# A selective-scan stage rebuilt: one scan per channel group over both state halves, one long buffer for inputs and states, products with C in pairs or trimmed

## The chip, the cores and the metric

The kernel runs on one core of one Trainium2 chip. The metric is the device time of one execution in microseconds (us); the number compared is the median over the timed runs of the same program. Five engines matter here and each works through its own queue in order: TensorE (PE in the profile, its weight loads PEld), VectorE (DVE), ScalarE (ACT), GpSimd (POOL) and SyncE (SP), which issues the DMAs.

## The reference, cut to what matters

The network has four layers. The first three (a gated Fourier block with attention, a Fourier mixing block with experts, a Hartley block) are not touched. The change lies in the fourth, which has two Mamba scans. For both, with `d_state = 16`:

```python
xz = x @ in_w.T
xi, z = jnp.split(xz, 2, axis=-1)
xc = silu(causal_conv(xi) + conv_b)
dt, Bm, Cm = jnp.split(xc @ xproj_w.T, ...)
dt = softplus(dt @ dt_w.T + dt_b)
dA = jnp.exp(dt[..., None] * A)
dBx = dt[..., None] * Bm[:, :, None, :] * xc[..., None]
h = dA_t * h + dBx_t                     # step over time
y = jnp.einsum('bds,bs->bd', h, C_t)
y = (y + xc * D) * silu(z)
return y @ out_w.T
```

The spectral scan ("spe") runs over 8 tokens per pixel, the spatial one ("spa") over all pixels of an image, row after row. Both results go through a group norm and a SiLU, are weighted and added to the layer's input.

## The kernel before

**Tiling.** The scans work in *units*. A spectral unit is 64 pixels of 8 tokens, 512 columns; there are 65. A spatial unit is up to `CR * CW` = 7 rows of 69 columns, 483 columns; an image has 19 of them: a first of 451 columns, 17 of 483 and a last of 170, and there are 4 images. A row's last column stands for a run of constant pixels; the state at the end of such a run comes from one small unit of 60 columns ("run") ahead of the images. The 64 x 2 inner channels and 16 states of a unit do not fit 128 partitions, so each unit is worked in 8 *steps* (`ORDER`, the channel groups q). A step has 128 partitions (channels by 8 states) and two state halves, `sg` 0 and 1.

**A step** takes these operations, for both halves:

- `do_exp` (L1484, ACT): dA = exp(dt * A), one instruction per half, into PSUM. Before, dA has four tiles of one PSUM bank (512 columns), two per step, so that steps take turns in two pairs.
- `do_dB` (L1500): dB = dx * B, both halves at once; for five of eight steps (`BY_DVE`) on DVE from PSUM, where PE has put dx (`do_sel`), for three on POOL from SBUF, where a DMA has put it. dB has its own tile for each q (two of them in a tile called `sr`).
- `do_scan` (L1505, DVE): h = dA * h + dB along the columns, one `tensor_tensor_scan` per half. In spatial units after the first of an image the scan starts from the state in the last column of the unit before.
- `do_hc` (L1532, POOL): hc = h * C for both halves. In spectral units the first of each 8 columns is left out (`do_first` does it by another formula).

**Around the steps**, per unit: `do_x` (PE, then on ACT a table load, two SiLUs and a table load back, L1412 to L1414), `do_dt` in nine parts (softplus out of Relu, Abs, Exp, Ln on ACT; its four terms are summed by PE into `v`, and part 7 copies `v` to dt on ACT, L1441), `do_bc` and `do_keep` (B and C by PE, copied by ACT, L1458), `do_sums` (PE adds hc over the states into y), `do_y` (DVE, yz = y * silu(z), L1557), the output projection. After an image, `combine` normalizes and adds in eight pieces, which lie among the next image's first eight units; each puts another two table loads and two SiLUs on ACT (L1765, L1766) and four copies on DVE (L1778).

**Order.** `scans` writes every operation with a due time in steps (`do(when, ...)`), sorts by it, and issues in that order under `manual_schedule`; equal due times keep the order in which they were written down. Each engine then works in that order and waits at semaphores. What follows names the steps of a unit 0 to 7 in the order in which they run. On ACT the block of `do_x` (due 3.1) lies between the exponentials of step 4 and of step 5 in both kernels. `do_sel` has one PSUM bank: step 0 of the next unit's dx is made (due 5.72) after the DVE has used that of step 7, and it lies on PE ahead of the four matmuls of `v` (due 5.95 to 6.7).

**Carry of the run state.** `keep_run` (L1624) copies the run's last state, per q on DVE, into every dB tile's run columns, once; dB's later writes leave these columns out.

Of the kernel before, what the change touches and what calls it, by code (L numbers as in the profile page):

```python
# [9 lines left out]
F32 = mybir.dt.float32  # L10
BF16 = mybir.dt.bfloat16
AF = mybir.ActivationFunctionType
ALU = mybir.AluOpType
# [4 lines left out]
NB, C, N = 4, 64, 128  # L18
# [5 lines left out]
KW = 65  # L24
ZC = 33
RUN = 60
# [7 lines left out]
CPX = 64  # L34
A1_SIZE = 10 * 4 * CPX + 96
# [277 lines left out]
class Net:  # L313
# [944 lines left out]
    def layer3(self, x2s, x2k, y1, ye):  # L1258
        tc, nc = self.tc, self.nc
        self.x2s, self.x2k, self.y1, self.ye = x2s, x2k, y1, ye  # L1260
        with ExitStack() as ctx:
# [8 lines left out]
            self.dA = [self.psum.tile([128, 512], F32, name=f"dA{i}") for i in range(4)]  # L1270
            self.const, self.small = const, pool("st", 2)
            self.hs = [const.tile([128, 2, 512], F32, name=f"h{q}") for q in range(8)]
# [5 lines left out]
            spare = self.held.tile([128, 32, C], F32, name="sr1").rearrange("p (i s a) c -> p i s (a c)", i=2, s=2)  # L1278
            self.dBs = [const.tile([128, 2, 512], F32, name=f"dB{q}") if q > 1 else spare[:, q] for q in range(8)]
# [8 lines left out]
            for u in us:  # L1288
                u["spa"], u["BC"] = u["kind"] != "spe", [None, None]
                u["c"] = self.consts("spa" if u["spa"] else "spe")  # L1290
# [186 lines left out]
    def do_exp(self, u, q, sg):  # L1477
# [3 lines left out]
        if sg == 0:  # L1481
            self.turn = 2 - self.turn
            u["dA", q] = self.dA[self.turn : self.turn + 2]
        self.nc.scalar.activation(t(u["dA", q][sg][:, u["lo"] : u["n"]]), t(u["dt", q]), AF.Exp, scale=a)  # L1484
# [11 lines left out]
    def do_dB(self, u, q, eng):  # L1496
        lo, dx, dB = u["lo"], u.pop(("dx", q)), self.dBs[q]
# [4 lines left out]
    def do_scan(self, u, q, sg):  # L1502
        lo, n, h = u["lo"], u["n"], self.hs[q][:, sg]
        init = h[:, u["before"] - 1 : u["before"]] if u["before"] else 0.0
        self.nc.vector.tensor_tensor_scan(h[:, lo:n], u["dA", q][sg][:, lo:n], self.dBs[q][:, sg, lo:n], init, ALU.mult, ALU.add)  # L1505
# [22 lines left out]
    def do_hc(self, u, q):  # L1528
        at = slice(u["lo"], u["n"])
        hc = self.work.tile([128, 2, 512], F32, name="hc", bufs=6)[:, :, at]  # L1530
        v = self.later(u, "p s (x t) -> p s x t")
        self.nc.gpsimd.tensor_tensor(v(hc), v(self.hs[q][:, :, at]), v(u["BC"][1][:, :, at]), ALU.mult)  # L1532
        u["hc", q] = hc

    def do_sums(self, u, i):
# [12 lines left out]
        v = self.later(u, "p (x t) -> p x t")  # L1548
        part, sg = divmod(i - 1, 2)
        for q in ORDER[4 * part : 4 * part + 4]:  # L1550
            r, h = divmod(q, 2)
            lhsT = self.c3["sum"][:, 32 * h : 32 * h + 32]
            self.mm(v(u["y"][32 * r : 32 * r + 32]), lhsT, v(u["hc", q][:, sg]), False, i == 4)
# [260 lines left out]
```

## Time and profile before

| what | value |
|---|---|
| timed runs | 7332.48, 7332.04, 7322.53 us; median 7332.04 |
| span of the profiled execution | 7327.9 us; no whole time of that one execution is listed, so it is set beside the median: 4.1 us less |
| scans start / spectral units end / last scan | about 3600 / 5260 / 7262 us of the span |
| engines busy over the whole span | PE 90%, DVE 74%, ACT 65%, POOL 49% |
| DVE scans (L1505) | 2272 instructions |
| POOL products with C (L1532) | 1128 instructions, 2453.5 us |
| spacing of spectral units | 25.58 us (64 spacings) |
| spacing of spatial units without `combine` | 25.27 us (44) |
| spacing of spatial units with `combine` | 27.9 us on average (24) |

The spacings are read off the starts of `dtx` (L1447), which POOL makes once per unit. In the profile, times are microseconds; a group's line has the source line, engine, operation, output and inputs with shapes, the count, the busy time and the mean of one in nanoseconds, and then the engine's idle time just before and what ended it. In a timeline the first column is the start, the second the length, and a bracket at the end gives idle time of that engine and its releaser. A DVE, ACT or POOL instruction's length includes a tail that overlaps the next one, so costs are better read as the distance from one start to the next.

### The profile page before, as it was taken

To read this page: it belongs to the slowest core of one execution; us is meant where nothing else is said; L and a number is where in the kernel's file an instruction comes from. 1 tells how busy PE (TensorE), PEld (TensorE's weight loads), DVE (VectorE), ACT (ScalarE), POOL (GpSimd) and SP (SyncE) were. 2 spreads that over 40 slices of the span, in tenths; PEclk is the share of its full clock that TensorE was granted. 3 is DMA by queue.
4 is the path that set the end of the run, shared out by engine and by line. 5 is a ranking of instruction groups with operands and counts; after the bars stand their busy time and mean duration, and the time that the engine had idled before them with its cause. 6 is when DMAs were issued, how large, how long until landed. Compare 5 with 4: busy or idle time off the path is not lost.

```text
span 7327.9 us, 106846 instructions
## 1 busy us (share of the span) xinstructions
PE 6630.8 (90%) x39058; PEld 2869.5 (39%) x39058; DVE 5405.7 (74%) x7737; ACT 4772.8 (65%) x7768; POOL 3608.7 (49%) x1908
## 2 busy tenths in 40 slices
PE   8998999989999899989899999999899888888897
PEld 6335553347434563346422332222322332332333
DVE  3665546564565646653599999999999899899896
ACT  2564635653455536552588888888788787887885
POOL 1000000000000000000399999999999899899896
PEclk9998989989999989987999999999999999999998
DMA  3000010002000010002455555555455465564554
GB/s 90 1 1 1 28 47 1 1 1 74 1 1 1 28 47 1 1 1 103 141 148 148 150 148 148 150 150 145 132 153 145 131 176 142 143 174 137 155 163 119
DMA packets 364112, 647.03 MB, mean 88 GB/s; under 512 B 46785, under 2 KB 219585, under 8 KB 362049
## 3 DMA queue, kind: packets, MB, share of 16 engines
q1 hardware_dynamic: 357680, 609.91, 30.3%
q10 hardware_dynamic: 5904, 30.28, 1.2%
q8 instruction: 308, 5.05, 0.3%
q14 instruction: 220, 1.79, 0.1%
HBM read 517.80 MB, written 122.22 MB: 87 GB/s over the span
## 4 chain that ended last, share of the span: by engine, by line
PE 49%; DVE 18%; issue 9%; POOL 9%; ACT 9%; DMA 4%; SPq 1%; POOLq 0%; DVEq 0%; ACTq 0%
PE ps_sp L331 14%; PE ps_m L331 9%; DVE h L1505 9%; PE ps_s L331 7%; PE ps_o L331 6%; POOL hc L1532 6%; PE ps_pt L331 4%; DVE dB L1500 3%; PE ps_y L331 3%; PE ps_dx L331 3%; DVE big L1059 2%; ACT dA L1484 2%; DMA s_dx<-ddx 2%; DMA big<-in_sr 1%; PE ps_m L809 1%
## 5 line engine op out<-in xcount | busy, mean ns | idle before, releaser
L1532 POOL TENSOR_TENSOR hc<-h,C 128x966 f32<-128x966 f32 (+3 forms) x1128 | 2453.5, 2276 | 119.7 <-DVE h L1505 92.6
L753 DVE TENSOR_REDUCE nmz<-ps_sp 128x1 f32<-128x320 f32 x2048 | 895.4, 485 | 622.7 <-PE ps_sp L331 613.4
L769 ACT ACTIVATE big<-ps_sp 128x512 f32<-128x512 f32 (+1 forms) x1536 | 830.7, 592 | 719.6 <-PE ps_sp L331 718.3
L928 POOL TENSOR_TENSOR aw<-pack_a 128x128 f32<-128x128 f32 x8 | 3.5, 461 | 2193.5 <-PE ps_m L331 2193.5
L1505 DVE TENSOR_TENSOR_SCAN h<-dA,h,dB 128x483 f32<-128x483 f32 (+2 forms) x900 | 1025.2, 1167 | 52.9 <-ACT dA L1484 52.9
L1505 DVE TENSOR_TENSOR_SCAN h<-dA,dB 128x512 f32<-128x512 f32 (+2 forms) x804 | 929.7, 1188 | 4.0 <-ACT dA L1484 4.0
L331 PE MATMUL ps_sp<-uT,kT 32*128 32x512 f32 x3072 | 924.2, 649 | 1.4 <-ACT big L769 0.8
L331 PE MATMUL ps_dx<-dtx,c_sel 128*128 128x483 f32 (+3 forms) x1420 | 752.7, 612 | 189.5 <-DVE dB L1500 188.3
L1484 ACT ACTIVATE dA<-s_dt,c_spa_a 128x483 f32<-128x483 f32 (+3 forms) x1232 | 760.7, 640 | 178.9 <-DVE h L1505 176.8
L331 PE MATMUL ps_sp<-kT,qT 32*128 32x320 f32 x4096 | 817.3, 499 | 3.9 <-ACT qT L734 3.3
L331 PE MATMUL ps_y<-hc,c_sum 128*32 128x483 f32 (+3 forms) x4512 | 683.7, 561 | 62.7 <-POOL hc L1532 58.0
L1484 ACT ACTIVATE dA<-s_dt,c_spe_a 128x448 f32<-128x448 f32 x1040 | 636.0, 632 | 155.2 <-DVE h L1505 154.3
L1500 POOL TENSOR_TENSOR dB<-s_dx,B 128x952 f32<-128x952 f32 (+6 forms) x300 | 672.6, 2244 | 14.6 <-DMA s_dx<-ddx 7.9
L1500 DVE TENSOR_TENSOR dB<-ps_dx,B 128x952 f32<-128x952 f32 (+4 forms) x600 | 646.0, 1079 | 14.5 <-PE ps_dx L331 13.7
L331 PEld LDWEIGHTS ps_dx<-dtx,c_sel 128*128 128x128 f32 x1420 | 225.4, 190 | 663.7 <-DVE dB L1500 225.4
L331 PEld LDWEIGHTS ps_sp<-uT,kT 32*128 32x128 f32 x3072 | 278.8, 185 | 438.0 <-issue 242.7
L331 PE MATMUL ps_o<-big,va 128*32 128x512 f32 (+1 forms) x3072 | 415.1, 612 | 0.0
L331 PE MATMUL ps_s<-pack_a,big 128*64 128x128 f32 (+4 forms) x2832 | 369.1, 306 | 44.8 <-DMA big<-in_x 19.8
L331 PEld LDWEIGHTS ps_sp<-kT,qT 32*128 32x128 f32 x4096 | 358.1, 190 | 57.2 <-issue 36.6
L331 PEld LDWEIGHTS ps_s<-pack_a,big 128*128 128x128 f32 (+2 forms) x2832 | 328.6, 180 | 66.3 <-issue 25.6
L1505 DVE TENSOR_TENSOR_SCAN h<-dA,h,sr 128x483 f32<-128x483 f32 (+2 forms) x300 | 342.6, 1162 | 0.0
L1500 POOL TENSOR_TENSOR sr<-s_dx,B 128x952 f32<-128x952 f32 (+2 forms) x150 | 336.6, 2246 | 0.3
(406 smaller groups left out, 10968.8 us busy)
## 6 DMA issues: line engine op xcount, KB each, us to landing
s_dt<-ddt SPq DMA_DIRECT2D x520, 256.0 KB
s_dt<-ddt SPq DMA_DIRECT2D x544, 241.5 KB
s_dx<-ddx SPq DMA_DIRECT2D x195, 256.0 KB
s_dx<-ddx SPq DMA_DIRECT2D x204, 241.5 KB
ddt<-dt SPq DMA_DIRECT2D x65, 256.0 KB
ddx<-dtx SPq DMA_DIRECT2D x65, 256.0 KB
A<-x2s SPq DMA_DIRECT2D x136, 121.2 KB
ddt<-dt SPq DMA_DIRECT2D x68, 241.5 KB
```

The source lines that it names most:

```text
L331: self.nc.tensor.matmul(out, lhsT, rhs, start=start, stop=stop)
L753: nc.vector.tensor_reduce(self.nmz[n % 2][:, j, at : at + 1], p[:, :KEYS], AX.X, ALU.max, negate=True)
L769: nc.scalar.activation(slot(m, 2 * wu + q)[rows], p[rows], AF.Exp)
L809: nc.tensor.transpose(p[:, 128 * j : 128 * j + 128], o[:, 128 * j : 128 * j + 128], k("ident"))
L928: nc.gpsimd.tensor_tensor(aw[i], k(f"aw{i + 1}"), k("sg"), ALU.mult)
L1059: nc.vector.scalar_tensor_tensor(acc(i), y, gate[:, p : p + 1], acc(i), ALU.mult, ALU.add)
L1484: self.nc.scalar.activation(t(u["dA", q][sg][:, u["lo"] : u["n"]]), t(u["dt", q]), AF.Exp, scale=a)
L1500: eng.tensor_tensor(v(dB[:, :, x:y]), v(d), v(u["BC"][0][:, :, x:y]), ALU.mult)
L1505: self.nc.vector.tensor_tensor_scan(h[:, lo:n], u["dA", q][sg][:, lo:n], self.dBs[q][:, sg, lo:n], init, ALU.mult, ALU.add)
L1532: self.nc.gpsimd.tensor_tensor(v(hc), v(self.hs[q][:, :, at]), v(u["BC"][1][:, :, at]), ALU.mult)
```

## The change

Two PSUM tiles of 1024 columns (two banks each) take the place of the four of 512, and steps alternate between them. One SBUF tile `all` has for each q one row of 1456 columns (`hd`) that holds both dB and the states. In spectral units dB is written to columns 0 to 1023 and one scan over 1024 columns overwrites it with h; the first column of each 8 has dA = 0, so nothing carries over from one half to the other. In spatial units after the first of an image one scan covers both halves with two carry columns: dA there is 0, and the dB buffer begins 483 columns behind the h buffer, so that the last state of the unit before is read as dB of the carry column. The scan then has 968 columns (655 in an image's last unit). The first unit of an image and the run keep two scans. Since states now overwrite dB's run columns of half 0, `keep_run` moves to ACT and restores them twice per spatial unit from `e_run`. Products with C are made on POOL for two steps at once in spectral units (1792 columns, three buffers for pairs in place of six), and in full spatial units without each row's last four columns (910 in place of 966); PE's sums then have 455 columns in place of 483. Due times: exponentials at -1.3 and -1.0 instead of -1.56 and -1.2, scan at 0.3 instead of 0.1 and 0.5.

```diff
-            self.dA = [self.psum.tile([128, 512], F32, name=f"dA{i}") for i in range(4)]
+            self.dA = [self.psum.tile([128, 1024], F32, name=f"dA{i}") for i in range(2)]
...
+            self.all = const.tile([128, 8, HD], F32, name="hd")
+            self.hd = {q: self.all[:, k] for k, q in enumerate(ORDER)}
...
-            self.turn = 2 - self.turn
-            u["dA", q] = self.dA[self.turn : self.turn + 2]
-        self.nc.scalar.activation(t(u["dA", q][sg][:, u["lo"] : u["n"]]), t(u["dt", q]), AF.Exp, scale=a)
+            self.turn = 1 - self.turn
+            u["dA", q] = self.dA[self.turn]
+        at = (TOK + 1) * sg + 1 if u["spa"] else 512 * sg
...
+        self.nc.scalar.activation(t(u["dA", q][:, at + u["lo"] : at + u["n"]]), t(u["dt", q]), AF.Exp, scale=a)
...
-    def do_scan(self, u, q, sg):
-        lo, n, h = u["lo"], u["n"], self.hs[q][:, sg]
-        init = h[:, u["before"] - 1 : u["before"]] if u["before"] else 0.0
-        self.nc.vector.tensor_tensor_scan(h[:, lo:n], u["dA", q][sg][:, lo:n], self.dBs[q][:, sg, lo:n], init, ALU.mult, ALU.add)
+    def do_scan(self, u, q):
+
+        scan = self.nc.vector.tensor_tensor_scan
+        lo, n, hd, dA = u["lo"], u["n"], self.hd[q], u["dA", q]
+        if not u["spa"]:
+            scan(hd[:, :1024], dA, hd[:, :1024], 0.0, ALU.mult, ALU.add)
+            return
+        if u["carried"]:
+            m = TOK + n + 2
+            scan(hd[:, :m], dA[:, :m], hd[:, TOK : TOK + m], 0.0, ALU.mult, ALU.add)
+            return
...
     def do_hc(self, u, q):
...
+        if u["spa"]:
+            at = slice(u["lo"], u["n"])
+            v = self.kept if u["carried"] and u["n"] == CR * CW else lambda t: t
+            mul(v(hc[:, :, at]), v(h[:, :, at]), v(c[:, :, at]))
+            return
+        if k % 2:
+            later = lambda t: t.rearrange("p i (x t) -> p i x t", t=8)[..., 1:]
+            h = later(self.all[:, k - 1 : k + 1, :1024])
...
-    def keep_run(self, u, q):
-        run = self.hs[q][:, :, RUN - 1].unsqueeze(2).to_broadcast([128, 2, CR])
-        self.nc.vector.tensor_copy(self.dBs[q][:, :, CW - 1 : CR * CW : CW], run)
+    def keep_run(self, u, part):
...
+        self.nc.scalar.copy(runs(0), self.e_run[:, at].to_broadcast([128, 4, CR]))
...
+            for part in range(2 if spa else 0):
+                do(4.1 * part + 4.6, self.keep_run, u, part)
...
-            do(-1.56, self.do_exp, u, q, 0)
-            do(-1.2, self.do_exp, u, q, 1)
+            do(-1.3, self.do_exp, u, q, 0)
+            do(-1.0, self.do_exp, u, q, 1)
...
-            do(0.1, self.do_scan, u, q, 0)
-            do(0.5, self.do_scan, u, q, 1)
-            if u["kind"] == "run":
-                do(0.55, self.keep_run, u, q)
-            else:
+            do(0.3, self.do_scan, u, q)
+            if u["kind"] != "run":
                 do(0.77, self.do_hc, u, q)
```

## Prediction

> **What bounds the kernel now.** I first read busy time by stretch, then, inside one unit, the timelines of POOL, DVE, ACT and PE. The stretches, columns PE, PEld, DVE, ACT, POOL busy, clock, DMA share, GB/s:
>
> ```profile
> 4000.00:4600.00 600.00, 548.80 (x2068) 179.65 (x2068) 578.64 (x564) 490.36 (x752) 600.00 (x306) 1.00 0.56 149
> 5450.00:5653.00 203.00, 183.98 (x610) 57.14 (x610) 193.40 (x182) 162.83 (x266) 203.00 (x98) 1.00 0.51 145
> 6300.00:6800.00 500.00, 435.38 (x1579) 155.36 (x1577) 456.32 (x494) 412.25 (x664) 465.54 (x237) 0.96 0.55 154
> ```
>
> In spectral units (first line) and in spatial units without `combine` (second) POOL has no idle time: it sets the 25.58 and 25.27 us per unit. DVE is at 96 and 95%. In the third stretch, where units with `combine` are mixed in, nobody is full, so something waits in a circle. POOL's starts give its prices:
>
> ```profile
> 4442.65 6.57 POOL L1532 TENSOR_TENSOR hc<-h,C 128x896 f32<-128x896 f32 x3
> 4448.94 2.60 POOL L1500 TENSOR_TENSOR sr<-s_dx,B 128x1024 f32<-128x1024 f32 x1
> 4451.27 1.51 POOL L1447 TENSOR_TENSOR dtx<-dt,xc 128x512 f32<-128x512 f32 x1
> ```
>
> Start to start: hc 2.10 us, dB 2.33, dtx 1.23. From 512 to 1024 columns that is 2.15 ns a column and 0.13 us fixed. Now ACT around `do_x`, and DVE beside it:
>
> ```profile
> 4402.55 0.64 ACT L1484 ACTIVATE dA<-s_dt,c_spe_a 128x448 f32<-128x448 f32 x1 [0.48 <-DVE h L1505]
> 4403.20 1.28 ACT L1412 ACT_TABLE_LOAD   x1
> 4404.49 1.20 ACT L1412 ACTIVATE xc<-ps_m,c_spe_cb 128x512 f32<-128x512 f32 x1
> 4405.48 1.16 ACT L1413 ACTIVATE zs<-ps_m 128x512 f32<-128x512 f32 x1
> 4406.65 1.28 ACT L1414 ACT_TABLE_LOAD   x1
> 4407.94 1.19 ACT L1484 ACTIVATE dA<-s_dt,c_spe_a 128x448 f32<-128x448 f32 x2
> ...
> 4412.55 0.62 ACT L1484 ACTIVATE dA<-s_dt,c_spe_a 128x448 f32<-128x448 f32 x1
> ...
> 4418.91 0.59 ACT L1441 COPY dt<-ps_m 128x512 f32<-128x512 f32 x1 [1.31 <-PE ps_m L331]
> ```
>
> ```profile
> 4400.20 2.31 DVE L1505 TENSOR_TENSOR_SCAN h<-dA,dB 128x512 f32<-128x512 f32 x2
> 4402.43 0.67 DVE L1557 TENSOR_TENSOR yz<-ps_y,zs 128x512 f32<-128x512 f32 x1
> 4403.01 1.21 DVE L1505 TENSOR_TENSOR_SCAN h<-dA,dB 128x512 f32<-128x512 f32 x1
> 4404.14 1.20 DVE L1500 TENSOR_TENSOR dB<-ps_dx,B 128x1024 f32<-128x1024 f32 x1
> ...
> 4408.62 1.22 DVE L1505 TENSOR_TENSOR_SCAN h<-dA,dB 128x512 f32<-128x512 f32 x1
> ...
> 4414.39 1.23 DVE L1500 TENSOR_TENSOR sr<-ps_dx,B 128x1024 f32<-128x1024 f32 x1 [1.20 <-PE ps_dx L331]
> ```
>
> Step 2's second scan ends at 4402.51. That frees the bank for step 4's second exponential (4402.55); then come 4.74 us of table loads and SiLUs, then step 5's first exponential, which ends at 4408.58. Step 5's first scan starts at 4408.62, just when DVE is free for it: slack zero. DVE's only idle time is 1.20 us before step 0's dB, behind PE, which waits for POOL. Where the ACT block is longer, with `combine`, the same place already costs time:
>
> ```profile
> 5920.52 1.22 DVE L1505 TENSOR_TENSOR_SCAN h<-dA,h,dB 128x483 f32<-128x483 f32 x1 [1.87 <-ACT dA L1484]
> ```
>
> **The change, part by part.** *Scans.* The scan's length rises from 252 ns (60 columns) to 1204 (512): 2.106 ns a column. Two of 512 are 2.24 us start to start; one of 1024 should be 2.20 (not under 2.16, columns alone; not over 2.24). Two of 483 with a state as start value are also 2.24, one of 968 is 2.08. Saved on DVE: 0.3 us per spectral, 1.3 per spatial unit. 1096 scans go. A scan across two banks is shown nowhere; I bound an extra price by zero and the 0.04 us fixed part.
>
> The Trainium skill (Perfetto Trace Analysis, "Optimizing Scalar/DVE Operations") gives about 125 ns per DVE instruction on PSUM and advises grouping where the engine is saturated; by that figure 1096 scans would be 137 us and the kernel at an estimated 7195. The rows above give 0.04 to 0.16 us each, and the saturated engine is POOL. The same section says that breaking instructions up may finish work sooner where an engine that isn't saturated causes bubbles in others, and that speaks against this change.
>
> *Products.* A pair saves one fixed part, 0.13 us (bounds 0 and 0.25, should 2 x 128 rows of 7 be worse or better): POOL 25.1 per spectral unit. Trimming 56 columns saves 0.12 us eight times: 24.3 per spatial unit. Rows with gaps cost nothing extra in dB (952 columns in rows of 68: 2.19 us).
>
> *Exponentials.* In the changed program step k's first exponential waits for the whole scan of step k-2, since a half is no tile of its own any more; the second also waits for the first to end (0.66 us start to start, as `sp_w` after `sp_u`, in place of 0.57). So after scan 2 ends ACT runs both exponentials of step 4, the block, and both of step 5, and only then scan 5 may start: 0.045 + 0.67 + 0.65 + 4.74 + 0.67 + 0.64 + 0.045 = 7.46 us. DVE's own work between is yz 0.58, scan 3 2.20, dB 1.12, scan 4 2.20, 0.08 of it already run: 6.02. Scan 5 is 1.4 us late, each unit.
>
> *Behind it.* Step 7's dB starts at 7.46 + 2.20 = 9.66. PE's `do_sel` for step 0, behind it, starts at 11.0 (length 1.20 and 0.14 to PE, as the dB at 4404.14 is followed by PE at 4405.48). From `do_sel` to the dt copy PE needs 5.68 (4413.23 to 4418.91), all matmuls back to back:
>
> ```profile
> 4413.23 1.13 PE L331 MATMUL ps_dx<-dtx,c_sel 128*128 128x512 f32 x2
> 4414.29 0.96 PE L331 MATMUL ps_y<-hc,c_sum 128*32 128x448 f32 x8
> 4415.18 1.13 PE L331 MATMUL ps_m<-sp_c,xht 128*128 128x512 f32 x2
> ```
>
> In the new order the dt copy (due 7.0) stands before step 0's second exponential (now also 7.0, written later; before, 6.8). So scan 0 starts at 11.0 + 5.68 + 0.49 + 0.64 + 0.045 = 17.85. From there to the next scan 2's end: three scans, two dB, 8.9. A spectral unit takes 26.8 us instead of 25.58; 64 of them: **+76**.
>
> If dt were not late: scan 6 waits for its second exponential, 4.04 us of ACT behind scan 5's (4409.13 to 4413.17), so 11.50; then five scans, three dB, y0: 14.6; unit 26.1: +34. That is the floor.
>
> *Spatial units without `combine`,* same sum with their rows (exponentials 0.70 apart with the wait, 0.68 to the load, block 3.74): scan 5 at 6.58, `do_sel` at 9.92, dt 5.50 later, scan 0 at 16.80, 8.4 more, unit 25.2 against 25.27; 44 of them: **-3**. Floor without the dt delay, and POOL's own work: 24.3, -43.
>
> *With `combine`:* from scan 1's end two exponentials and a copy, 4.17 of loads and SiLUs, two exponentials, 3.73, two exponentials: scan 5 at 12.5, scan 0 at 22.7, unit 28.4 against 27.9; 24 of them: **+12** (without the dt delay 27.6: -7).
>
> *`keep_run`.* Two small copies on ACT per unit; the nearest row is the 0.18 us ACT instruction on 7 columns, I take 0.2. The first waits for step 3's product and is reached 8.0 us after scan 2; POOL ends that product between 4.7 (straight after scan 3) and 6.8 (behind its own queue), so it waits for nothing. If POOL were later, exponential 6 behind the copy, and with it scan 6, would be late by as much. POOL's dB for the next step 1 waits for the copy, a product lies between. DVE loses its eight copies in the run unit: nothing. SP's queue keeps its DMAs and their order. An image's last unit scans 655 columns (1.42 us) in place of twice 170 (0.54 us each): up to 4 x 8 x 0.4 = 13 us if DVE binds there; 17 us pass in that unit for some 14 of DVE work, so I take 0.
>
> Sum: 76 - 3 + 12 = +85 on the profiled span of 7327.9: 7413; with the 4.1 us by which the median of the runs lies above it, **7417**. POOL has slack then (25.1 of 26.8), so its gains don't show.
>
> **The rivals.**
>
> - *Floor:* PE gets from scan 5 to dt sooner by 0.7 us or more, so that dt is in time. +34 - 43 - 7 = -16: 7316. For: PE no longer waits for a late POOL. Against: the 5.68 us hold no wait, and dx has one bank.
> - *ACT keeps ahead (the other side):* POOL remains the bound and its savings count: 64 x 0.5 + 44 x 0.97 = -75: 7257. It decides if scan 2 to scan 5 on ACT stays within 6.0 us. Against: zero slack at 4408.62 and 1.87 us at 5920.52.
> - *Pairs are slow:* POOL's unit is four pairs and 8.8 us (three dB, dtx, bb 0.60), so it binds again when a pair takes over 4.5 us in place of 2 x 2.10 - 0.13 = 4.07. Each 0.1 us beyond is 4 x 64 x 0.1 = 26 us; at 4.8 us 7417 + 77 = 7494. Against: rows of 7 already run at (2.10 - 0.13) / 896 = 2.2 ns a column.
> - *More waits:* yz follows dB 3 by one scan only, where PE took 2.5 us from dB 3 to the sums (4399.15 to 4401.64), so yz and the next unit's matmuls slip by 0.4 us; hidden in scan 5's wait until it passes that by another 0.3. At 0.5 us in each of 132 units 7417 + 66 = 7483.
>
> **How the numbers follow.** Forecast 0.72 (its own range 7380 to 7455), floor 0.09, ACT ahead 0.05, slow pairs 0.07, more waits 0.07. The range 7340 to 7480 leaves out the next two and the far half of the last two, 0.2 together. The measurement tells about 0.2%, 15 us. The floor lies just past it, so half of it counts as same: faster 0.10, same 0.06, slower 0.84.
>
> **What would show it.** Right: DVE idle before scans by ACT's dA (now none in spectral units) of 1.4 and more per unit, scan 0 released by the exponential behind the dt copy, POOL no longer at 600 of 600, unit spacing 26.8, 25.2, 28.4; scan 2.20 and 2.08, pair 4.07, trimmed product 2.08 us. Wrong: a spectral spacing under 25.6, or POOL still full.

## The result and the profile after

The changed kernel takes 7570.34 us (median; 7564.79 to 7575.03) against 7332.26 for the kernel before in the runs beside it: 1.0327 times as long, 95% interval 1.0313 to 1.0342. The forecast was 7417, its range ended at 7480: the direction was right, the size was not. The profiled execution has a span of 7562.9 us, 235.0 more than before's.

The same three stretches as before, columns PE, PEld, DVE, ACT, POOL busy, granted clock, DMA share, GB/s:

```profile
4000.00:4600.00 600.00, 514.11 (x1936) 171.52 (x1934) 538.07 (x349) 460.15 (x703) 550.28 (x198) 0.97 0.51 139
5450.00:5653.00 203.00, 170.57 (x576) 55.42 (x574) 178.09 (x113) 158.55 (x268) 189.88 (x93) 0.95 0.49 138
6300.00:6800.00 500.00, 408.47 (x1494) 148.37 (x1486) 419.58 (x337) 397.93 (x664) 424.30 (x224) 0.94 0.52 144
```

POOL is no longer full (550 of 600 instead of 600) and DVE fell from 96 to 90% in spectral units: every engine now waits for another. The clock column (the share of full speed that TensorE was granted) fell too, from 1.00 to 0.97 and 0.95 in the first two rows. The prediction printed that column and drew nothing from it.

Where the waits lie, from the list of costly groups (behind the bar: busy us, mean ns, then the engine's idle time just before and what ended it):

```profile
L1564 POOL TENSOR_TENSOR hc<-hd,C 128x910 f32<-128x910 f32 (+3 forms) x868 | 2316.0, 2677 | 362.3 <-DVE hd L1529 147.5
L1529 DVE TENSOR_TENSOR_SCAN hd<-dA,hd 128x968 f32<-128x968 f32 (+1 forms) x576 | 1226.3, 2131 | 188.7 <-ACT dA L1490 185.9
L333 PE MATMUL ps_dx<-dtx,c_sel 128*128 128x483 f32 (+3 forms) x1420 | 796.1, 644 | 589.9 <-DVE hd L1518 589.5
L1525 DVE TENSOR_TENSOR_SCAN hd<-dA,hd 128x1024 f32<-128x1024 f32 x520 | 1185.2, 2283 | 109.7 <-ACT dA L1490 100.5
```

DVE's scans wait 286 us for ACT, as forecast. PE waits 589.5 us for DVE's dB at `do_sel`, three times the 188.3 us of before.

**One unit.** ACT, DVE and PE in the unit that the prediction worked through and at the start of the next (a timeline: start, length, and in brackets the idle time and its releaser):

```profile
4405.12 1.31 ACT L1490 ACTIVATE dA<-s_dt,c_spe_a 128x448 f32<-128x448 f32 x2 [1.24 <-DVE hd L1525]
4406.44 1.28 ACT L1415 ACT_TABLE_LOAD   x1
...
4411.20 1.31 ACT L1490 ACTIVATE dA<-s_dt,c_spe_a 128x448 f32<-128x448 f32 x2
...
4421.68 0.58 ACT L1444 COPY dt<-ps_m 128x512 f32<-128x512 f32 x1 [2.09 <-PE ps_m L333]
...
4430.03 0.58 ACT L1461 COPY C<-ps_m 128x512 f32<-128x512 f32 x1 [3.18 <-PE ps_m L333]
...
4435.70 1.19 ACT L1415 ACTIVATE xc<-ps_m,c_spe_cb 128x512 f32<-128x512 f32 x1 [0.96 <-PE ps_m L333]
```

```profile
4402.80 2.28 DVE L1525 TENSOR_TENSOR_SCAN hd<-dA,hd 128x1024 f32<-128x1024 f32 x1
...
4412.54 2.29 DVE L1525 TENSOR_TENSOR_SCAN hd<-dA,hd 128x1024 f32<-128x1024 f32 x1 [0.83 <-ACT dA L1490]
...
4416.63 2.29 DVE L1525 TENSOR_TENSOR_SCAN hd<-dA,hd 128x1024 f32<-128x1024 f32 x1 [0.69 <-ACT dA L1490]
...
4422.84 2.29 DVE L1525 TENSOR_TENSOR_SCAN hd<-dA,hd 128x1024 f32<-128x1024 f32 x1 [0.43 <-ACT dA L1490]
...
4429.56 2.28 DVE L1525 TENSOR_TENSOR_SCAN hd<-dA,hd 128x1024 f32<-128x1024 f32 x1
4433.84 0.69 DVE L1605 TENSOR_TENSOR yz<-ps_y,zs 128x512 f32<-128x512 f32 x1 [2.00 <-PE ps_y L333]
...
4440.51 2.29 DVE L1525 TENSOR_TENSOR_SCAN hd<-dA,hd 128x1024 f32<-128x1024 f32 x1 [0.47 <-ACT dA L1490]
```

Scan 2 (4402.80) ends at 4405.08. Step 4's exponentials start 0.04 later, the block and step 5's exponentials follow, and scan 5 starts at 4412.54, 7.46 us behind scan 2: the forecast's 7.46. Scan 6 waits for its exponential (4.09 behind scan 5; 4.04 forecast). Scan 0 starts at 4422.84, released by the exponential behind the dt copy, 10.30 behind scan 5 (10.39 forecast). The chain is there, link by link.

What the chain did not hold is on PE, where this unit passes into the next:

```profile
4416.00 1.12 PE L333 MATMUL ps_dx<-dtx,c_sel 128*128 128x512 f32 x2 [0.52 <-DVE hd L1518]
...
4422.34 1.88 PE L333 MATMUL ps_m<-xc,c_spe_bc 128*128 128x512 f32 x4
4426.30 2.08 PE L333 MATMUL ps_dx<-dtx,c_sel 128*128 128x512 f32 x2 [2.08 <-DVE hd L1518]
4428.17 2.63 PE L333 MATMUL ps_m<-xc,c_spe_bc 128*128 128x512 f32 x4
```

The same dx matmul takes 1.12 us elsewhere, the same B and C matmul 1.88. Three stretches around it (columns as above):

```profile
4415.94:4426.20 10.26, 8.22 (x24) 3.03 (x24) 9.14 (x8) 7.45 (x14) 9.15 (x4) 1.00 0.45 134
4426.20:4429.60 3.40, 3.30 (x4) 1.51 (x5) 3.40 (x4) 0.64 (x1) 3.40 (x3) 0.51 0.87 189
4429.60:4436.40 6.80, 6.80 (x35) 1.89 (x33) 4.80 (x4) 5.36 (x8) 6.80 (x3) 1.00 0.69 192
```

After PE had waited 2.08 us for DVE's dB, its clock was half for 3.4 us (a drop, in what follows). What stands behind on PE comes late: C's copies (ACT idle 3.18 us; 1.52 one unit earlier), the x matmuls (xc idle 0.96; none earlier), the sums (yz idle 2.00; 0.43 earlier). So in this next unit scan 5 (4440.51) comes 8.67 us behind the end of scan 2 (4431.84), not 7.46.

The 57 steady spectral units of this trace, from one scan 2's end to the next, are of three kinds. In 28 no drop meets the chain: 26.7 to 26.8 us, as forecast. In 24 a drop follows the wait for step 2's dB: yz waits 2.0 to 2.1 us for PE, xc 0.96 to 1.13, scan 5 comes 8.7 to 8.8 us behind scan 2, and the unit takes 27.9 to 28.0. In 5 the drop falls on the dx matmul behind z: scan 0 comes 11.4 us behind scan 5 instead of 10.30, and the unit takes 27.7. Plain spatial spacings are of two kinds: 9 of 38 at 25.1 to 25.2, as forecast, and 29 at 26.7 to 26.9. Between 3600 and 5260 us the time at half clock is 106 us in the changed kernel and 14 before; from 5260 to 7300 it is 259 and 167; from 3600 to the end of the last scan, 410 and 161.

**Where the 235 us lie,** from the spacings of `dtx` (here 61 steady spectral spacings, 38 between units without and 21 between units with `combine`):

| | before, us | after, us | sum, us |
|---|---|---|---|
| spectral units | 25.58 | 27.33 | +107, and +6 in the first three |
| spatial without `combine` | 25.28 | 26.40 | +43 |
| spatial with `combine` | 27.91 | 29.61 | +36 |
| images' ends, run, first units (18) | | | +38 |
| ahead of the first and behind the last | | | +6 |

The spectral spacings of `dtx` are not even: most alternate between 26.1 to 26.4 and 28.3 to 28.6 us, and two of them make 54.6 us, which is sixteen times 3.413 us.

### The profile page after: what moved, and what is told of

The parts are those of the page before. It is cut to its first block, busy times and chain, and to the rows that moved or that the text cites. A ratio compares the mean times of both kernels' runs of the same rounds, so it can differ in the third digit from the quotient of the medians.

```text
span 7562.9 us, 105294 instructions
## 1 busy us (share of the span) xinstructions
PE 6622.1 (88%) x39058; PEld 2887.9 (38%) x39058; DVE 5344.1 (71%) x6633; ACT 4813.2 (64%) x7926; POOL 3524.4 (47%) x1648
## 4 chain that ended last, share of the span: by engine, by line
PE 56%; DVE 19%; ACT 11%; issue 7%; POOL 4%; DMA 3%; SPq 0%; DVEq 0%; POOLq 0%; ACTq 0%
PE ps_sp L333 13%; PE ps_m L333 12%; PE ps_s L333 7%; PE ps_o L333 6%; PE ps_dx L333 6%; DVE hd L1518 5%; DVE hd L1525 5%; PE ps_pt L333 4%; PE ps_y L333 4%; ACT dA L1490 3%; DVE hd L1529 3%; POOL hc L1564 2%; DMA big<-in_sr 2%; DVE big L1061 2%; ACT L1417 1%
## 5 line engine op out<-in xcount | busy, mean ns | idle before, releaser
L1564 POOL TENSOR_TENSOR hc<-hd,C 128x910 f32<-128x910 f32 (+3 forms) x868 | 2316.0, 2677 | 362.3 <-DVE hd L1529 147.5
L1529 DVE TENSOR_TENSOR_SCAN hd<-dA,hd 128x968 f32<-128x968 f32 (+1 forms) x576 | 1226.3, 2131 | 188.7 <-ACT dA L1490 185.9
L333 PE MATMUL ps_dx<-dtx,c_sel 128*128 128x483 f32 (+3 forms) x1420 | 796.1, 644 | 589.9 <-DVE hd L1518 589.5
L1525 DVE TENSOR_TENSOR_SCAN hd<-dA,hd 128x1024 f32<-128x1024 f32 x520 | 1185.2, 2283 | 109.7 <-ACT dA L1490 100.5
L1518 POOL TENSOR_TENSOR hd<-s_dx,B 128x1024 f32<-128x1024 f32 (+5 forms) x450 | 956.4, 2126 | 95.1 <-ACT hd L1681 78.5
L1518 DVE TENSOR_TENSOR hd<-ps_dx,B 128x1024 f32<-128x1024 f32 (+5 forms) x750 | 810.9, 1081 | 33.2 <-PE ps_dx L333 31.7
L1490 ACT ACTIVATE dA<-s_dt,c_spa_a 128x483 f32<-128x483 f32 (+3 forms) x1232 | 788.9, 645 | 44.9 <-DVE hd L1529 30.6
L333 PE MATMUL ps_y<-hc,c_sum 128*32 128x455 f32 (+3 forms) x4512 | 548.6, 556 | 3.2 <-POOL hc L1564 3.2
L333 PE MATMUL ps_s<-pack_a,big 128*64 128x128 f32 (+4 forms) x2832 | 371.6, 307 | 43.7 <-DMA big<-in_x 20.2
L333 PE MATMUL ps_m<-xc,c_spa_bc 128*128 128x483 f32 (+3 forms) x616 | 313.1, 631 | 0.0
L1461 ACT COPY C<-ps_m 128x483 f32<-128x483 f32 (+4 forms) x284 | 159.5, 562 | 211.7 <-PE ps_m L333 210.9
```

The costliest lines, as they stand in the source:

```text
L333: self.nc.tensor.matmul(out, lhsT, rhs, start=start, stop=stop)
L1461: self.nc.scalar.copy(u["BC"][k // 2][:, k % 2, u["lo"] : u["n"]], u["bc", k])
L1490: self.nc.scalar.activation(t(u["dA", q][:, at + u["lo"] : at + u["n"]]), t(u["dt", q]), AF.Exp, scale=a)
L1518: eng.tensor_tensor(v(dB[:, :, x:y]), v(d), v(u["BC"][0][:, :, x:y]), ALU.mult)
L1525: scan(hd[:, :1024], dA, hd[:, :1024], 0.0, ALU.mult, ALU.add)
L1529: scan(hd[:, :m], dA[:, :m], hd[:, TOK : TOK + m], 0.0, ALU.mult, ALU.add)
```

## The experiments

**Theory A:** the two-bank dA tile makes a loop over DVE, ACT and PE (26.8 us per spectral unit, 25.2 in plain spatial ones, as forecast), and that loop lets PE idle so long that its clock falls, which adds the rest. **Rivals:** B, PE's order is late whatever its clock is; D, the products' part causes the loss; and, later, that the due times, the long scan, `keep_run` or ACT's order do.

All numbers, with the mean spacings from each profile (spectral / without `combine` / with) and the time at half clock between 3600 and 7300 us (the same window for all, so that it leaves out the last units of the slower kernels):

| kernel | time, us | spacings, us | half clock, us |
|---|---|---|---|
| before | 7332 | 25.58 / 25.28 / 27.91 | 182 |
| after | 7570 | 27.33 / 26.40 / 29.61 | 365 |
| two added matmuls | 7557 | 27.29 / 25.48 / 30.66 | 321 |
| z over 128 rows | 7574 | 27.29 / 26.37 / 29.90 | 352 |
| both | 7492 | 26.68 / 25.37 / 30.20 | 150 |
| dt copy later | 7515 | 27.09 / 25.81 / 28.91 | 333 |
| no table loads (after) | 7567 | 27.30 / 26.35 / 29.92 | 420 |
| products as before | 7592 | 27.31 / 26.52 / 30.08 | 369 |
| before, new due times | 7331 | 25.57 / 25.27 / 27.82 | 195 |
| before, tile and due times | 7496 | 27.32 / 25.35 / 29.52 | 340 |
| before, products | 7281 | 25.21 / 24.53 / 27.92 | 221 |

**1. Keep PE's clock up.** First with two matmuls of zero weights (`FILL` is 2) where PE waits for step 2's dB; `self.open` is the unit whose y PE is summing:

```diff
         self.mm(u["bc", k], u["c"]["bc"][:, 128 * k : 128 * k + 128], u["xc"])
+        if k == 1 and self.open:
+            for _ in range(FILL):
+                self.mm(self.open["y"][0:32], self.zero, self.open["zs"], False, False)
```

> The changed kernel, with two matmuls of zero weights put on PE where it waits for step 2's dB (they add nothing to y). Theory A (the clock): the changed kernel's loop is 26.8 us per spectral unit by its waits, as predicted, and the rest comes from PE running at half clock for 3.41 us whenever it idled for most of the 3.41 us before. Then the time at granted clock 0.5 in 3600 to 5260 us falls from 106 us to under 35, spectral units are 26.8 us each without the alternation of 26.2 and 28.4, plain spatial units come to 25.2, and the whole to 7430 to 7470 us against 7570. Rival B (the order on PE: what stands behind do_sel is late whatever the clock is): spacing and time stay, 7570 within 15.

7557.33 us, ratio 1.0301 to before. Plain spatial units did what A said (29 of the 38 spacings lie at 25.1 to 25.2). Spectral units stayed at 27.3, which B had said, but not for B's reason: the half clock was still there, 133 us of it, and had moved. PE and the clock, in the unit of this kernel:

```profile
4415.52 1.12 PE L334 MATMUL ps_m<-A,c_spe_z 64*128 64x512 f32 x2
4417.92 1.41 PE L334 MATMUL ps_dx<-dtx,c_sel 128*128 128x512 f32 x2 [1.28 <-DVE hd L1522]
4419.27 1.97 PE L334 MATMUL ps_m<-yz,c_spe_ow 128*64 128x512 f32 x2
```

```profile
4415.16:4418.57 3.41, 2.13 (x6) 0.59 (x4) 3.41 (x3) 3.38 (x4) 3.41 (x2) 1.00 0.85 243
4418.57:4421.98 3.41, 3.41 (x5) 0.79 (x4) 2.58 (x2) 2.73 (x4) 3.41 (x2) 0.50 0.03 7
```

In the first of the two stretches PE was busy 2.13 of 3.41 us, and still the clock fell in the next. A third of the stretch was z, a matmul on 64 of 128 rows. Hence the second edit, in which z takes all 128 rows, the added weights zero:

```diff
-        self.mm(v(pz), c["z"][64:128], a2[64:128])
+        self.mm(v(pz), c["z"], a2)
...
+            nc.vector.memset(c3[s + "_z"][0:64], 0.0)
```

> The changed kernel, with the matmul of z over 128 rows in place of 64, the added weights zero; the same columns, so the same time on PE at the same clock. In the run with two added matmuls the half clock moved to the dx matmul behind z, after 3.41-us stretches that were idle for 0.37 only, of which z on 64 of 128 rows filled a third. Theory A2: what sets the clock is work weighed by its share of the 128 rows, with the border near 0.47 of a 3.41-us stretch. Then this alone takes away the drops behind z and leaves those behind the long wait for dB (about 2 us): spectral units stay near 27.3 us and the time within 7540 to 7575. Theory A1 (only idle time counts): no change at all in the number of drops.

7573.85 us: no gain alone, as expected. Drops behind the long wait stay. Both edits together, without the added matmuls in units with `combine`:

> The two matmuls of zero weights in the long wait and z over 128 rows together; the two matmuls are left out where the output of the image before is combined, since there they stood in PE's way (12 of those units took 30 to 33 us in the run with them everywhere, 2 without). Theory A2: time at half clock in spectral units falls from 106 us to under 30, their spacing to 26.1 to 26.8 without alternation (33 to 77 us less), plain spatial units to 25.2 (some 50 less), combine units stay: 7450 to 7495. Theory A1 (only idle time counts): the drops behind z stay as with the two matmuls alone, spectral 27.3, 7520 to 7560. Theory B (order on PE, not its clock): the clock rises and the spacing stays at 27.3 and 26.5, 7570.

7492.20 us, ratio 1.0217 (1.0200 to 1.0234): 78 us back. PE in the same place, and the spectral stretch:

```profile
4421.71 1.02 PE L334 MATMUL ps_m<-xht,c_spe_z 128*128 128x512 f32 x2
4424.21 1.10 PE L334 MATMUL ps_dx<-dtx,c_sel 128*128 128x512 f32 x2 [1.47 <-DVE hd L1523]
4425.23 1.07 PE L334 MATMUL ps_m<-yz,c_spe_ow 128*64 128x512 f32 x2
```

```profile
3600.00:5260.00 1660.00, 1499.19 (x5678) 495.71 (x5679) 1519.90 (x987) 1305.71 (x1987) 1547.30 (x561) 1.00 0.52 141
```

PE idles a little longer behind z (1.47 us), and its matmuls keep full speed: the row count of z decided. Half clock in the spectral part is 7 us instead of 106. The spacing there is 26.68 us and, first units included, the spectral part costs 74 us more than before, where the prediction had 76. On DVE, from scan 2's end to the next, all its steady units take 26.66 to 26.69 us, with scan 5 at 7.46 and scan 0 at 17.76. Plain units have 25.1 in most places, where it had 25.2. So B falls, and so does the view that only idle time counts. The spacings of `dtx` still vary between 26.1 and 27.2 us without any drop; since DVE's units are even, that variation is of POOL's place for `dtx` alone.

**2. The dt copy behind step 0's second exponential.**

```diff
-            do(-1.0, self.do_exp, u, q, 1)
+            do(-1.02, self.do_exp, u, q, 1)
```

> The changed kernel, with one due time altered: the second exponential of a step at -1.02 in place of -1.0, so that on ACT the dt copy comes behind the second exponential of the next unit's step 0. Theory A: the unit has a chain through dt of 26.8 us and one without it of 26.1; scan 0 is then no longer released by an exponential behind dt, and 0.7 us per spectral and 0.9 per spatial unit go (100 us over the 132), less what the clock gives back: 7480 to 7550. Rival C (the dt copy is only late because something else on PE is, and that bounds the unit): the spacing stays at 27.3, time 7570 within 15.

7515.06 us, inside A's range: 55 us for the delay that the prediction had priced at 0.7 to 0.9 us per unit (some 100), with the half clock little changed (333 us in place of 365). In spectral units it gave only 0.24 us, where 0.7 was priced.

**3. The products' part,** alone on the kernel before, and taken out of the changed kernel:

```diff
-        hc = self.work.tile([128, 2, 512], F32, name="hc", bufs=6)[:, :, at]
+        if k % 2 == 0:
+            u["hcs"] = self.work.tile([128, 2, 2, 512], F32, name="hc", bufs=3)
...
+            mul(later(u["hcs"].rearrange("p i s x -> p i (s x)")), h, cc)
```

> The kernel before, with the products' part of the change alone (pairs in spectral units, trimmed in spatial ones; scans, dA and dB as before). Theory A: POOL is the bound of the kernel before, so its savings count: 0.5 us for each of 64 spectral and 0.97 for each of 44 plain spatial units, 75 us, 7257 (7245 to 7285). Rival D: ACT, which had no slack at scan 5 in the trace before, or a pair that comes too late for the sums, takes the gain: 7320 to 7340.

> The changed kernel with products as before the change (each step by itself, 896 and 966 columns). POOL is then at 25.6 of 27.3 us per spectral unit and 25.3 of 26.4 in spatial ones. Theory A: products are hidden in the loop's slack, 7570 within 20. Rival D (the pairs or the trimming are part of the loss): 7500 or less. Rival E (POOL's saving shows already): 7600 or more.

Alone the products make the kernel faster than both: 7280.54 us, ratio 0.9924 (0.9907 to 0.9940), 54 us of A's 75. The stretches of this kernel, columns as above:

```profile
4000.00:4600.00 600.00, 548.98 (x2083) 181.58 (x2082) 587.73 (x572) 499.40 (x762) 596.59 (x214) 1.00 0.56 151
5450.00:5653.00 203.00, 183.81 (x628) 58.75 (x620) 199.70 (x188) 168.62 (x273) 203.00 (x101) 1.00 0.54 149
```

POOL is still all but full and DVE at 98%: where POOL bounds, its savings count, 0.37 and 0.75 us per unit. In the changed kernel they hide: without them it takes 7591.92, 22 us more. That is 2 us beyond the range that A gave, so they show a little. D falls.

**4. ACT's block.** Relu in place of the SiLUs in spectral units takes two table loads out of the block between the exponentials of steps 4 and 5 (and makes the spectral scan another one).

```diff
-        nc.scalar.activation(w(u["xc"]), v(p), AF.Silu, bias=c["cb"])
-        nc.scalar.activation(w(u["zs"]), v(pz), AF.Silu)
-        nc.scalar.preload_act_table_set("natural_log_exp_and_others")
+        F = AF.Silu if first else AF.Relu
+        nc.scalar.activation(w(u["xc"]), v(p), F, bias=c["cb"])
+        nc.scalar.activation(w(u["zs"]), v(pz), F)
```

> The changed kernel, with Relu in place of the two SiLUs of do_x in all spectral units but the first, so that their two table loads go (the spectral scan's output is another one). The block on ACT between the exponentials of steps 4 and 5 shrinks from 4.74 to about 2.2 us. Theory A: scan 5 then waits until 4.9 us behind scan 2, and DVE has 6.0 us of its own work, so ACT no longer holds it; the loop falls to what DVE and POOL need, 25.0 to 25.5 us per spectral unit, PE no longer idles long and keeps its clock: 64 times 1.9 to 2.3 us less, 7425 to 7450. If the two-bank scan were late through something else than this block, the spacing would stay above 26.5 and the time above 7515.

> The same edit on the kernel before, as a control. POOL is full there in spectral units, so without the tables the spacing stays at 25.58 us within 0.1 and the time at 7335 within 12. If ACT was part of the bound before, up to 1 us per unit goes, 7270.

The control stayed (7331.15). The changed kernel stayed too, at 7567.20 with 27.30 us: a clear miss of A. DVE in that kernel:

```profile
4407.44 2.29 DVE L1528 TENSOR_TENSOR_SCAN hd<-dA,hd 128x1024 f32<-128x1024 f32 x1 [1.57 <-ACT dA L1493]
...
4424.18 0.69 DVE L1608 TENSOR_TENSOR yz<-ps_y,zs 128x512 f32<-128x512 f32 x1 [2.12 <-PE ps_y L333]
```

Scan 5 waits no more. In its place scan 6 waits 1.57 us (before the edit 0.69) for an exponential that stands behind softplus on ACT, and yz 2.12 us for PE, which is at half clock for 147 us in the spectral part, 41 more than with the tables. So the block is one link of the loop and not its only price. No run keeps this kernel's clock, but its trace holds units without a drop: 16 of 57 take 26.1 to 26.4 us, the others 27.6 to 27.9. So without drops the block would be worth some 0.6 us (26.7 to 26.1), an estimate from these units; the drops hide it, and A's 25.0 to 25.5 is not reached.

**5. Which part makes the loop.** The tile alone on the kernel before, first with the old due times:

```diff
-            self.dA = [self.psum.tile([128, 512], F32, name=f"dA{i}") for i in range(4)]
+            self.dA = [self.psum.tile([128, 1024], F32, name=f"dA{i}") for i in range(2)]
```

> The kernel before, with only the four one-bank dA tiles made two two-bank tiles (two scans per step, due times and products as before). An exponential then waits for both scans of the step two back. Theory A: step 5's first exponential ends 0.045 + 0.67 + 0.57 + 4.74 + 0.60 = 6.6 us behind scan 2's end, where DVE's own work (yz 0.58, two steps of scans 4.48, dB 1.12) takes 6.2: scan 5 is late by 0.4 to 0.5 us in each spectral unit. POOL, which is full, must take that up, so 25.6 to 26.1 us per unit and 7330 to 7370: the tile alone is not the loss, the whole scan and the late dt copy behind it make the larger part. Rival F (the tile is the loss): 26.5 and more per unit, 7430 and above.

8413.99 us, far from both. This is no measure of the tile: with the old due times the first exponential of step k (-1.56) is written down ahead of the second scan of step k - 2 (-1.5). As the two halves are now one tile, that scan takes the tile to be rewritten and waits for the exponential, and the exponential waits for the first scan. ACT and DVE take turns in each step (one such scan waits 3.27 us for ACT; 33.2 us per spectral unit). With the new due times this goes:

> The kernel before with the changed due times of the exponentials alone (-1.3 and -1.0), four one-bank tiles and two scans per step kept. On ACT the dt copy comes ahead of step 0's second exponential. Theory A: scan 0's second half is then released by that exponential, 16.5 us behind scan 2's end, and 7.9 us of scans and dB follow: 24.4 us, less than POOL's 25.58, so no change: 7332 within 15. Rival J (the due times are the loss): 26.5 us and more per spectral unit, 7400 and above.

> The kernel before with two two-bank tiles and the changed due times, but two scans per step and products as before. Theory A: an exponential waits for both scans of the step two back and the first scan for both exponentials; scan 5 comes 7.3 to 7.5 us behind scan 2's end as in the changed kernel, scan 0 some 17.6 us, and 8.9 us follow: 26.4 to 26.8 us per spectral unit as in the changed kernel, and more where PE's clock drops, 7440 to 7580. Then the tile, not the long scan, is the loss. Rival K (the whole scan is needed for it): 25.6 to 26.0, 7330 to 7370.

The due times alone cost nothing (7330.84, ratio 0.9997, 0.9988 to 1.0007). Tile and due times together, with two scans per step, make 7495.63 us (ratio 1.0220) and the same 27.32 us per spectral unit as the whole change. DVE there shows the same two waits:

```profile
4417.08 1.22 DVE L1505 TENSOR_TENSOR_SCAN h<-dA,dB 128x512 f32<-128x512 f32 x1 [1.27 <-ACT dA L1484]
...
4421.17 1.22 DVE L1505 TENSOR_TENSOR_SCAN h<-dA,dB 128x512 f32<-128x512 f32 x1 [0.62 <-ACT dA L1484]
```

So in spectral units the loss is the tile's: half a step can no longer be freed or released by itself. The rival that the whole scan is needed for it falls. That the mean is 27.32 here and 27.33 in the whole change says little by itself, since ten different kernels of this case share it (see the last section); what counts is that this kernel's units without a drop (27 of 56) take 26.4 to 26.9 us and the others 27.8 to 27.9, much as in the changed kernel. Plain spatial units lose hardly anything by the tile (25.35); their 1.1 us come with the rest of the change, and go again when PE's clock is kept (25.37 in the run with both edits).

**6. Units with `combine` and the images' ends.** C's second copy behind the combine block; the last unit in two scans; no `keep_run` in later units; yz behind the scan of step 3:

```diff
-                do(when + 0.59, self.do_keep, u, k)
+                do(when + (1.1 if spa and k == 3 else 0.59), self.do_keep, u, k)
```

> The changed kernel, with the second copy of C on ACT moved behind the two SiLUs of combine, to just ahead of step 4's exponentials, in spatial units. In units with combine this copy waited 0.99 us for PE in front of the second exponential of step 3 and of the combine block; scan 5 came 13.6 us behind scan 1's end where the prediction had 12.5. Theory G (ACT in order: its wait for PE is the missing 1.1 us): these units fall from 29.5 to 28.4 to 28.7 us, and the time by 20 to 27 us, to 7543 to 7552. Theory H (PE is late for other reasons and meets ACT at the next place): 29.5 stays, 7570 within 8.

```diff
-        if u["carried"]:
+        if u["carried"] and n == CR * CW:
             m = TOK + n + 2
```

> The changed kernel, with an image's last unit (170 columns) scanned half by half from the carried state, as its first unit is, in place of one scan over 655 columns. The prediction put these longer scans (8 times 0.9 us of DVE work per image) at nothing, up to 13 us. If they are the reason that this unit takes 20.2 us in place of 16.6 to 17.5, it comes back to under 18 and the time falls by 8 to 13 us (7557 to 7562). If PE or ACT sets that unit, 20.2 stays and the time is 7570 within 5.

```diff
-            for part in range(2 if spa else 0):
+            for part in range(2 if u["kind"] == "run" else 0):
```

> The changed kernel without keep_run's restoring copies on ACT in the spatial units (it runs in the run unit only, so that later units' run columns of half 0 hold other numbers). The prediction put these copies at nothing; in the changed kernel ACT stood 72 to 78 us idle at them, waiting for POOL. Theory A: what follows on ACT there is an exponential that DVE doesn't need yet, so nothing: 7570 within 12. Rival L (this wait delays the exponentials of steps 2 and 3 and C's copies, and through them the combine block): 0.3 us and more in each of 76 spatial units, 7545 and below.

```diff
-                do(10.76, self.do_y, u)
+                do(11.32, self.do_y, u)
```

> The changed kernel, with yz on DVE behind the scan of step 3 in place of ahead of it. Theory A: yz's wait for PE (2.0 us in the units behind a drop of the clock) lies in the 1.4 us by which scan 5 waits for ACT anyway, and the late x matmuls, not yz, pass PE's delay on; 0 to 0.6 us in half of the units, 7550 to 7573. Rival B (yz is the link by which PE's order holds DVE): 0.6 us and more in every unit, 7490 or less.

In the changed kernel a unit with `combine` had this on ACT and DVE:

```profile
5972.31 0.56 ACT L1461 COPY C<-ps_m 128x483 f32<-128x483 f32 x1 [0.99 <-PE ps_m L333]
```

```profile
5968.45 2.16 DVE L1529 TENSOR_TENSOR_SCAN hd<-dA,hd 128x968 f32<-128x968 f32 x1
...
5984.15 2.17 DVE L1529 TENSOR_TENSOR_SCAN hd<-dA,hd 128x968 f32<-128x968 f32 x1 [2.88 <-ACT dA L1490]
```

Scan 1 (5968.45) ended at 5970.61, so scan 5 came 13.54 us later instead of 12.5; 0.99 of the difference is that copy. It is 13.5 in all 21 of these units (the first of each image left out). With the copy moved away it is 12.5 to 12.8 in all of them, so the mechanism of G is shown. The time is 7564.29 all the same, not told apart from the changed kernel's, and the mean spacing 29.32. The traces say where the gain went: in 9 of the 21 units the clock is full between scan 5 and the next scan 1 (half for 0.5 us at most), and they take 28.3 us from scan 1 to scan 1 (28.4 was forecast; 29.3 to 29.5 in the changed kernel). In the other 12 a drop lies there, and they take 30.0 to 31.5. In one of them ACT and PE had this:

```profile
6034.20 0.56 ACT L1444 COPY dt<-ps_m 128x483 f32<-128x483 f32 x1 [4.55 <-PE ps_m L333]
```

```profile
6025.77 1.98 PE L333 MATMUL ps_dx<-dtx,c_sel 128*128 128x483 f32 x2 [2.64 <-DVE hd L1518]
```

The dt copy waits 3.0 to 4.6 us for PE in these 12 units and 1.3 to 1.6 in the 9. In the changed kernel it waits 3.0 us and more in 3 of the 21 only (31.0 us each).

The last unit in two scans takes 19.2 us instead of 20.2, so DVE is a third of its excess at most, and the time (7566.71) cannot show 4 us. Without `keep_run` 7568.70: ACT's idle time there (112 us in the changed kernel's profile, waiting for POOL's dB) is off the path. yz later gives 24 us (7546.62), 3 us more than A allowed and far less than B asked; in the profile 14 us of it lie in plain spatial units and 5 at the images' ends, in spectral units under 1.

**7. All mends together,** and the best kernel's variant:

> The changed kernel with everything found so far: two matmuls of zero weights in PE's long wait, z over 128 rows, the dt copy behind step 0's second exponential, C's second copy behind the combine block, the last unit in two scans. Theory A: spectral units at the floor of 26.1 (64 times 1.2 less than the changed kernel), plain spatial units under 25.2, units with combine 28.2 to 28.7: 7375 to 7430, still slower than before since ACT's block between the exponentials stays. If the parts meet at the same place, only the clock's 78 us remain, 7470 to 7495.

> The kernel with all mends (7435 us), and yz on DVE behind the scan of step 3. Theory A: with PE's clock kept yz waits only 0.4 to 0.5 us for PE in a spectral unit, and scan 5 waits 0.7 us for ACT just after, which takes that up: 7435 within 10. Rival B (PE's order still holds DVE through yz): 0.4 us per unit and more, 7385 or less.

> The kernel before, with pairs and trimmed products, z over 128 rows and C's second copy behind the combine block in spatial units. Theory G: ACT's wait for PE at that copy (0.92 us in the trace before) is on the path of units with combine there too; 24 times 0.5 to 1 us less than with the products alone, 7255 to 7270. Theory H: PE sets those units, 7280 within 8.

7435.06 us (26.39 / 25.13 / 29.23), 5 us above A's range, and with yz later 7425.94, ratio 1.0127 (1.0112 to 1.0142), just inside what A gave there. With everything found, the two-bank version is still slower than before. Of the products with z over 128 rows and the later copy of C: 7276.45, ratio 0.9921 (0.9906 to 0.9936), not told apart from the products alone, as H said.

## Why the prediction was wrong, point by point

- **ACT's chain through the two-bank tile** (scan 5 at 7.46, scan 0 at 17.85 behind scan 2): right, measured 7.46 and 17.76. With PE's clock kept every steady spectral unit takes 26.67 us on DVE where 26.8 stood, the term of +76 measures +74, and most plain spatial units take 25.1 where 25.2 stood.
- **PE without a wait and at one speed: the step that failed.** The prediction took PE's durations from a kernel in which PE hardly waited ("from `do_sel` to the dt copy PE needs 5.68, all matmuls back to back"), and let ACT's block (4.74) and yz (0.58) between scan 2 and scan 5 run with no wait for PE. The sum has no term for the 2.08 us that PE waits for step 2's dB in every spectral unit of the changed kernel, nor for the half clock that follows. Where no drop came, its numbers held (5.68 from 4416.00 to the dt copy at 4421.68). In 24 of 57 units a drop put scan 5 at 8.7 to 8.8 instead of 7.46, in 5 it lengthened the part from `do_sel` to the dt copy. The profile of before had evidence of such drops: the clock column of its third stretch, in which an image's end and units with `combine` lie, reads 0.96. The terms came out as +113 instead of +76, +43 instead of -3; keeping the clock gives back 78 us of the 153 missed.
- **The dt copy was priced too high,** which the sum does not show: with PE's clock kept, moving it takes a spectral unit from 26.67 to 26.38 us, 0.29 and not 0.7, so the floor of 26.1 is 26.4 (scan 6 comes 4.28 us behind scan 5 on average, not 4.04).
- **With `combine`: +36 for +12** (21 of 24 units). The chain from scan 1's end was 13.5, not 12.5. The prediction listed the two exponentials and the copy ahead of the block without asking whether the copy's input was there; it waits 0.8 to 1.0 us for PE. With the copy moved, and where no drop comes, the forecast holds (28.3).
- **Images' ends taken at nothing: +38.** 9 us of it lie in the last units, for whose scans 13 us were named as a bound; 1.0 us per image came back when those scans were made in two. The rest is spread over the other spacings at the ends, and stays open.
- **More waits:** the rival had yz's delay right for units without a drop (0.43 us, 0.4 forecast); behind a drop it is 2.0 to 2.1. A chance of 0.07 and a price that stopped at 0.5 us per unit were too little: the clock was not in it.
- **Products and scans:** a pair takes 4.04 us start to start (4.07 forecast), a scan of 1024 columns 2.20, of 968 columns 2.08. All as forecast; no extra price for two banks, and slow pairs fall. The estimate of 7195 from the Trainium skill's figure per instruction (Perfetto Trace Analysis, "Optimizing Scalar/DVE Operations") is far off here: the measured time lies 375 us above it. The same section says that breaking instructions up may let work finish sooner where an engine that isn't saturated causes bubbles in others. That points the right way, but no run here tests it: with the tile and the due times alone 163 us are lost with as many scans as before, so the joined waits cost, not the longer instruction. POOL had slack, so the gain was hidden, as said: 22 us of the 54 that the products give alone.
- **`keep_run` at nothing:** right in time, wrong in its reason. It does wait, 112 us in all, for POOL's dB and not for the product that was named, where nobody behind it is in a hurry.

About half of the miss is the clock, shown by giving it back. Of the 24 us missed in units with `combine`, the copy accounts for some 20 (21 times 1.0, an estimate from the chain's 13.5 and 12.5). The 38 us at the images' ends are only partly explained, and not shown to be one cause.

## What to carry to other kernels

Joining two half tiles saves instructions, but it also joins their waits; where a producer and a consumer take turns with two buffers, the half is what lets each run ahead, and the joined tile must be priced as a loop over all engines, not by instructions saved. When an edit makes TensorE wait inside a loop that it used to fill, price its matmuls at half speed for some 3.4 us after such a wait (here behind two waits of 2.08 us in five), and read the clock column of before to see where that happens already. A matmul on half of the rows counted like half a load in these traces. And split a change that touches two engines: here the part that relieved the full engine was worth 0.8%, and the other part lost 3% to 4% on top of it.

## What the runs showed of the hardware

In each trace the drops of the clock start on one grid of 3.413 us. Of the 1311 drops in the twenty traces of this case (3650 to 7250 us) 1074 last one of its stretches, 144 two, the others three to five, one eleven. The load of a stretch is here PE's busy time in it by the profile, each matmul weighed by the share of the 128 rows that it uses. Of the 19334 stretches at full clock, all 861 with a load under 0.40 were followed by half clock, 429 of 806 from 0.40 to 0.50, 19 of 17667 above, and none of the 17158 above 0.55. Without the weights 114 of 826 stretches with a load of 0.60 to 0.65 were followed by a drop; with them none of 701 is. On the chip, z over 128 rows in place of 64 took such drops away (half clock in the spectral part 133 us with the two added matmuls alone, 7 with both edits). That the weighing is exactly by rows is a reading that fits, not a measurement of it. Back to full clock more is needed: of the stretches at half clock, 1193 of 1208 in which PE was busy for at least 0.97 were followed by full clock, and none of 229 in which it was busy for less than half.

The Trainium skill (TensorE: Matmul & The Clock Gate, Part 1) describes a free-running window of 4096 cycles at 1.2 GHz, 3413 ns, and the traces agree with that length. Its table there gives the half rate after at least one idle window, and its section "Why this matters for your kernels" advises against gaps of more than some 3 us. Here gaps of 2.08 us were enough, and 1.28 us behind a matmul on half of the rows; the measurement decides.

A loop can settle on that grid: two spectral units of the changed kernel take 54.6 us, sixteen stretches, and about every second unit is hit. Ten of the kernels, with quite different edits, share a mean spectral spacing of 27.29 to 27.33 us, and eight stretches are 27.31. So a spacing that does not move after an edit need not mean that the edit was without effect: look at the units without a drop.
